# A feed-forward loop that turns half of its features with DMA transposes, as pairs of float16 numbers, in an order written out for four engines

## The chip, the cores and the metric

The kernel runs on one core of a Trainium2 chip. A core has five engines that run side by side, each with its own queue of instructions: TensorE (PE in the profile: matrix products and transposes, with weight loads shown apart as PEld), VectorE (DVE), ScalarE (ACT), GpSimd (POOL) and SyncE (SP, which here only issues DMA transfers). They meet through semaphores. The metric is device time of the whole kernel in microseconds (us), the median of several runs.

## The reference

Two layers of a graph attention followed by a feed-forward part, over 4096 rows of 256 features. The change concerns the feed-forward part of the first layer, which starts from the layer-normed rows and repeats one step thirty times:

```python
def step(h, _):
    h = h + 0.01 * jnp.tanh(h)
    h = h * jax.nn.sigmoid(h)
    h = _layernorm(h, ln_w, ln_b)
    h = jnp.einsum('bsc,dc->bsd', h, W) + b
    return (h, None)
x, _ = jax.lax.scan(step, x, None, length=N_ITERS)   # N_ITERS = 30, 256 features
```

Rows are independent of each other; within a row each step needs the one before. All of it is float32.

## The kernel before, in words

The program is one long function, `gnn_ffn_kernel`: attention of layer 0, the feed-forward stage that is changed here, two attentions of layer 1, and a mixture of experts. Outside of stages with a written order the Tile framework's scheduler decides the order of instructions on each engine.

In the feed-forward stage all 4096 rows stay in SBUF as `y`, at a hundred times their value. They are worked on in 8 groups (`NG`) of 512 rows: 128 partitions by 4 rows (`G`) by 256 features. One group in one step is a unit, so there are 30 x 8 = 240 units, and unit `u` needs the result of unit `u` - 8. The loop over `at` is a software pipeline: one pass starts unit `at`, and carries on with units `at` - 1, `at` - 2 and `at` - 3. A unit goes through these steps:

- ScalarE: tanh of `y` into `th` (L759). GpSimd: `th` + `y` (L760), called the sum below. ScalarE: silu of it into `z` (L765).
- VectorE: mean and variance of the 4 rows of `z` (`over_std`: bn_stats L101, bn_aggr L103), + EPS (L105); GpSimd: to the power -1/2 (L106). The mean itself isn't needed, since `wT` has its own column mean taken off (L741).
- TensorE: 8 transposes of 128x128 that turn `z` (L114, in `transposed`) into PSUM; ScalarE copies them into `zT` (L800).
- TensorE: for each of the 4 rows two float32 products of 128x128 by 128x256, accumulated in PSUM as `po` (L774).
- VectorE: `y` = `po` x rstd + bias, one instruction for each of the 4 rows (L784). In the last step also `t` = 0.01 `y` + `t` (L794), the residual, which is then stored.

`init(g)` (L697 and following) norms the rows of group `g` and scales them into `y`; it runs in the first passes, one group per pass. The weights are prepared on the side, before the loop (L711 to L741).

Of the kernel before, what the change touches and what calls it, by code (L numbers as in the profile page):

```python
# [11 lines left out]
F32 = mybir.dt.float32  # L12
BF16 = mybir.dt.bfloat16
F16 = mybir.dt.float16
I32 = mybir.dt.int32
AF = mybir.ActivationFunctionType
OP = mybir.AluOpType
AX = mybir.AxisListType
# [3 lines left out]
P = 128  # L22
C = 256
KC = C // P
# [3 lines left out]
G = 4  # L28
EPS = 1e-5
# [6 lines left out]
TINY = 1e-30  # L36


def bcast_rows(ap, n=P):

    return bass.AP(tensor=ap.tensor, offset=ap.offset, ap=[[0, n]] + [list(x) for x in ap.ap])
# [3 lines left out]
def gnn_ffn_kernel(ctx: ExitStack, tc: tile.TileContext, a: dict, out: bass.AP):  # L45
    nc = tc.nc
# [3 lines left out]
    NG = NT // G  # L50
    GR = G * P
# [44 lines left out]
    def over_std(pool, src):  # L96

        st = pool.tile([P, G, 6], F32, name="ln_st")
        mv = pool.tile([P, G, 2], F32, name="ln_mv")
        for r in range(G):  # L100
            nc.vector.bn_stats(st[:, r, :], src[:, r, :])  # L101
        for r in range(G):
            nc.vector.bn_aggr(mv[:, r, :], st[:, r, :])  # L103
        rstd = pool.tile([P, G], F32, name="ln_rstd")
        nc.vector.tensor_scalar(rstd, mv[:, :, 1], EPS, None, op0=OP.add)  # L105
        nc.gpsimd.tensor_tensor(rstd, rstd, mhalf, OP.pow)  # L106
        return rstd, mv

    def transposed(psum, src, name="tp"):

        ps = psum.tile([P, KC, GR], F32, name=name)
        for k in range(KC):
            for r in range(G):
                nc.tensor.transpose(ps[:, k, r * P : (r + 1) * P], src[:, r, k * P : (k + 1) * P], ident)  # L114
        return ps
# [560 lines left out]

    with ExitStack() as scope:
        one = scope.enter_context(tc.tile_pool(name="f_one", bufs=1))  # L680
        wT = one.tile([P, KC, C], F32, name="wT")
        bias = one.tile([P, C], F32, name="bias")
        last = one.tile([P, C], F32, name="last")
        y = one.tile([P, NT, C], F32, name="y")
        work = scope.enter_context(tc.tile_pool(name="f_work", bufs=3))
        small = scope.enter_context(tc.tile_pool(name="f_small", bufs=6))

        x1 = {}

        def load(g):  # L690
            if g not in ahead:
                load_ahead(x1d, g)
            x1[g] = ahead.pop(g)

        def init(g):
            t = x1.pop(g)
            rstd, mv = over_std(small, t)  # L697
            rs = small.tile([P, G], F32, name="rs")
            nc.vector.tensor_scalar(rs, rstd, 100.0, None, op0=OP.mult)
            nm = small.tile([P, G], F32, name="nm")  # L700
            nc.vector.scalar_tensor_tensor(nm, mv[:, :, 0], -1.0, rs, op0=OP.mult, op1=OP.mult)
            for r in range(G):
                nc.scalar.activation(
                    y[:, g * G + r, :], t[:, r, :], AF.Identity, scale=rs[:, r : r + 1], bias=nm[:, r : r + 1]
                )

        load(0)
        load(1)
        with tc.tile_pool(name="f_prep", bufs=1) as prep, tc.tile_pool(name="f_pps", bufs=1, space=PSUM) as pps:
            ln = prep.tile([2 * KC, P], F32, name="ln")  # L710
            nc.scalar.dma_start(ln[:KC], a["L0_ffn_ln_w"].rearrange("(k p) -> k p", p=P))  # L711
            nc.scalar.dma_start(ln[KC:], a["L0_ffn_ln_b"].rearrange("(k p) -> k p", p=P))
            wr = prep.tile([P, KC, C], F32, name="wr")
            nc.scalar.dma_start(wr, a["L0_ffn_W"].rearrange("(k p) c -> p k c", p=P))
            nc.scalar.dma_start(bias, bcast_rows(a["L0_ffn_b"]))
            init(0)
            ps = pps.tile([P, 2 * KC], F32, name="ps_ln")
            nc.tensor.transpose(ps, ln, ident[: 2 * KC, : 2 * KC])
            lnT = prep.tile([P, 2 * KC], F32, name="lnT")
            nc.vector.tensor_scalar(lnT, ps, 100.0, None, op0=OP.mult)  # L720
            lbb = prep.tile([P, KC, P], F32, name="lbb")
            nc.vector.tensor_copy(lbb, lnT[:, KC:, None].to_broadcast([P, KC, P]))
            ps = pps.tile([P, KC, C], F32, name="ps_w")
            for k in range(KC):
                for o in range(KC):
                    nc.tensor.transpose(ps[:, k, o * P : (o + 1) * P], wr[:, o, k * P : (k + 1) * P], ident)
            raw = prep.tile([P, KC, C], F32, name="raw")
            nc.vector.tensor_copy(raw, ps)
            ps = pps.tile([P, C], F32, name="ps_b")
            for k in range(KC):  # L730
                nc.tensor.matmul(ps, lbb[:, k, :], raw[:, k, :], start=(k == 0), stop=(k == KC - 1))
            nc.vector.scalar_tensor_tensor(bias, bias, 100.0, ps, op0=OP.mult, op1=OP.add)

            nc.vector.tensor_scalar(last, bias, -100.0, None, op0=OP.add)
            for k in range(KC):
                nc.vector.tensor_scalar(raw[:, k, :], raw[:, k, :], lnT[:, k : k + 1], None, op0=OP.mult)
            ps = pps.tile([P, C], F32, name="ps_m")
            for k in range(KC):
                nc.tensor.matmul(ps, mean, raw[:, k, :], start=(k == 0), stop=(k == KC - 1))
            for k in range(KC):  # L740
                nc.vector.tensor_tensor(wT[:, k, :], raw[:, k, :], ps, OP.subtract)  # L741

        ps_t = scope.enter_context(tc.tile_pool(name="f_pst", bufs=2, space=PSUM))
        ps_o = scope.enter_context(tc.tile_pool(name="f_pso", bufs=2, space=PSUM))

        th, zs, rs, zT = {}, {}, {}, {}
        units = FFN_STEPS * NG
        for at in range(units + 4):
            if at < NG:
                if at + 2 < NG:  # L750
                    load(at + 2)
                if at:
                    init(at)
            if units - NG <= at - 1 < units:
                load((at - 1) % NG)
            if at < units:
                g = at % NG
                th[at] = work.tile([P, G, C], F32, name="th")
                nc.scalar.activation(th[at], y[:, g * G : (g + 1) * G, :], AF.Tanh, scale=0.01)  # L759
                nc.gpsimd.tensor_tensor(th[at], th[at], y[:, g * G : (g + 1) * G, :], OP.add)  # L760
            if 0 <= at - 2 < units:
                pt = transposed(ps_t, zs.pop(at - 2))
            if 0 <= at - 1 < units:
                z = zs[at - 1] = work.tile([P, G, C], F32, name="z", bufs=4)
                nc.scalar.activation(z, th.pop(at - 1), AF.Silu, scale=0.01)  # L765
                rs[at - 1] = over_std(small, z)[0]
            if 0 <= at - 3 < units:
                u = at - 3
                g = u % NG
                src = zT.pop(u)  # L770
                po = ps_o.tile([P, G, C], F32, name="po")
                for r in range(G):
                    for k in range(KC):
                        nc.tensor.matmul(  # L774
                            po[:, r, :],
                            src[:, k, r * P : (r + 1) * P],
                            wT[:, k, :],
                            start=(k == 0),
                            stop=(k == KC - 1),
                        )  # L780
                rstd = rs.pop(u)
                end = u >= units - NG
                for r in range(G):
                    nc.vector.scalar_tensor_tensor(  # L784
                        y[:, g * G + r, :],
                        po[:, r, :],
                        rstd[:, r : r + 1],
                        last if end else bias,
                        op0=OP.mult,
                        op1=OP.add,  # L790
                    )
                if end:
                    t = x1.pop(g)
                    nc.vector.scalar_tensor_tensor(  # L794
                        t, y[:, g * G : (g + 1) * G, :], 0.01, t, op0=OP.mult, op1=OP.add
                    )
                    nc.sync.dma_start(rows_of(x2d, g), t)
            if 0 <= at - 2 < units:
                zT[at - 2] = work.tile([P, KC, GR], F32, name="zT")
                nc.scalar.copy(zT[at - 2], pt)  # L800


    RH = a["L1_ffn_router_w1"].shape[1]
# [456 lines left out]
```

## Time and profile before

| | us |
|---|---|
| median of 3 runs (lowest, highest) | 3557.42 (3556.58, 3568.16) |
| the profiled execution, and its span | 3558.91, 3557.2 |
| feed-forward stage, first tanh to the end of the last L794 | 823.9 to 1905.0 |
| L774 products in the stage: busy, mean of one | 874.1, 0.381 |
| L114 transposes, all of the kernel: busy, mean of one | 250.8, 0.274 |
| L760 sums: busy, mean of one | 567.5, 2.366 |

The profile is one execution taken by the hardware profiler. "Busy" is the time in which an engine had an instruction under way; a line such as "L784 DVE" names the source line and the engine, then the output and inputs with their shapes. What stands in brackets with "<-" is the idle time of the engine just before, and what it waited for. A matmul's duration is modelled and matmuls overlap, so distances from start to start say more than durations; a float32 product has two records.

### The profile page before, as it was taken

What the parts mean: (1) busy time and instruction counts of PE and PEld (TensorE: products, weight loads), DVE (VectorE), ACT (ScalarE), POOL (GpSimd) and SP (SyncE); (2) the same over time, 40 slices, a digit from 0 to 9 for tenths busy, and PEclk for the clock granted to TensorE, in tenths of its full rate; (3) what the DMA queues carried; (4) which work ended last, traced back from release to release, by engine and by line L of the source; (5) the groups of instructions that cost most, each with busy time, mean ns of one, the idle gap of its engine ahead of it and who ended that gap; (6) DMA issues with size and microseconds to landing.
All of it is one profiled execution on the core that took longest, in us unless ns stands there. A gap on an engine that the chain in (4) does not pass through costs nothing. (4 is left out here: it accounts for less than half of the span.)

```text
span 3557.2 us, 80784 instructions
## 1 busy us (share of the span) xinstructions
PE 3272.9 (92%) x33523; PEld 2963.8 (83%) x33523; DVE 3010.9 (85%) x6039; ACT 2613.4 (73%) x2902; POOL 1101.7 (31%) x899
## 2 busy tenths in 40 slices
PE   6889999996999999999998899999979999995995
PEld 5778888885888888888887799999869999993784
DVE  6899999997887877778787799999989999997445
ACT  2688888895766666666663799999879999992221
POOL 3210101004877777777772000000000000001662
PEclk8899999998999999999998899999999999997997
DMA  6796886602000000000006021313221331314224
GB/s 137 139 234 134 196 189 139 189 17 60 1 1 1 1 1 1 1 1 1 1 1 220 14 92 50 123 30 113 79 97 46 111 120 37 120 37 148 90 90 182
DMA packets 280200, 288.47 MB, mean 81 GB/s; under 512 B 97149, under 2 KB 230426, under 8 KB 279834
## 3 DMA queue, kind: packets, MB, share of 16 engines
q1 hardware_dynamic: 198770, 224.18, 19.2%
q0 software_dynamic: 73920, 52.97, 9.7%
q10 hardware_dynamic: 7144, 6.16, 0.6%
q8 instruction: 264, 4.33, 0.5%
q14 instruction: 102, 0.84, 0.1%
HBM read 248.01 MB, written 68.81 MB: 89 GB/s over the span
## 5 line engine op out<-in xcount | busy, mean ns | idle before, releaser
L556 PE MATMUL acc<-vals,m 128*128 128x130 f16 (+1 forms) x19456 | 1723.4, 233 | 83.0 <-DVE m L619 42.7
L470 ACT ACTIVATE st<-f1b,f2b 128x1024 bf16<-128x1024 f32 (+2 forms) x1664 | 1659.4, 1073 | 100.1 <-DVE m L604 92.1
L556 PEld LDWEIGHTS <-m 128*128 128x128 bf16 x19456 | 1518.3, 98 | 181.3 <-DVE m L619 64.9
L604 DVE TENSOR_TENSOR m<-st,m 128x2048 bf16<-128x2048 bf16 (+2 forms) x832 | 929.0, 1134 | 12.4 <-ACT st L470 12.3
L774 PE MATMUL po<-wT,zT 128*128 128x256 f32 x3840 | 874.1, 381 | 13.3 <-ACT zT L800 12.3
L774 PEld LDWEIGHTS po<-wT,zT 128*128 128x128 f32 x3840 | 713.6, 191 | 104.2 <-ACT zT L800 14.8
L556 PE MATMUL acc<-vals,rows 128*128 128x130 f16 x5120 | 614.1, 221 | 15.1 <-DVE rows L619 15.1
L760 POOL TENSOR_TENSOR th<-th,y 128x1024 f32<-128x1024 f32 x240 | 567.5, 2366 | 192.8 <-ACT th L759 192.2
L106 POOL TENSOR_TENSOR ln_rstd<-ln_rstd,mhalf 128x4 f32<-128x4 f32 x272 | 282.4, 1039 | 881.6 <-DVE ln_rstd L105 676.4
L556 PEld LDWEIGHTS <-rows 128*128 128x128 bf16 x5120 | 490.0, 96 | 20.5 <-DVE rows L619 20.1
L101 DVE BATCH_NORM_STATS2 ln_st<-z 128x6 f32<-128x256 f32 x960 | 338.0, 414 | 190.5 <-ACT z L765 190.5
L800 ACT COPY zT<-tp 128x1024 f32<-128x1024 f32 x240 | 242.7, 1011 | 323.8 <-PE tp L114 323.8
L619 DVE TENSOR_TENSOR rows<-m,m 128x2048 bf16<-128x2048 bf16 x320 | 391.7, 1224 | 10.2
L784 DVE SCALAR_TENSOR_TENSOR y<-po,ln_rstd,bias 128x256 f32<-128x256 f32 x928 | 378.8, 470 | 6.6 <-PE po L774 5.9
L765 ACT ACTIVATE z<-th 128x1024 f32<-128x1024 f32 x240 | 254.5, 1060 | 17.4 <-POOL th L760 17.4
L114 PE MATMUL tp<-ident,z 128*128 128x128 f32 x1920 | 250.8, 274 | 8.8 <-ACT z L765 7.9
L114 PEld LDWEIGHTS tp<-ident,z 128*128 128x128 f32 x1920 | 225.3, 141 | 35.5 <-ACT z L765 10.5
L759 ACT ACTIVATE th<-y 128x1024 f32<-128x1024 f32 x240 | 251.3, 1048 | 4.8 <-DVE y L784 4.7
L209 POOL DMA_DIRECT2D rows<-in_adj_dram x80 | 72.9, 912 | 497.3 <-PE tp_m L219 488.2
L619 DVE TENSOR_TENSOR m<-m,m 128x1792 bf16<-128x1792 bf16 (+1 forms) x200 | 202.2, 1011 | 13.0 <-PE acc L556 0.5
L449 POOL MEMSET hs<- 128x4 f32 x3 | 0.3, 102 | 607.2 <-DVE u L500 585.9
L307 PE MATMUL ph<-g_w,xT 128*128 128x264 f32 x384 | 120.0, 477 | 30.9 <-DVE v L377 27.4
(212 smaller groups left out, 2319.7 us busy)
## 6 DMA issues: line engine op xcount, KB each, us to landing
m<-edges SPq DMA_DIRECT2D x32, 2048.0 KB, 9.9
rows<-in_adj_dram POOLq DMA_DIRECT2D x64, 448.0 KB
edges<-ms SPq DMA_DIRECT2D x64, 448.0 KB, 5.0
m<-edges SPq DMA_DIRECT2D x16, 1792.0 KB
f1b<-fd SPq DMA_DIRECT2D x32, 512.0 KB, 3.4
rows<-x1d SPq DMA_DIRECT2D x16, 512.0 KB, 6.3
y<-yd SPq DMA_DIRECT2D x16, 512.0 KB, 9.5
f1b<-fd SPq DMA_DIRECT2D x16, 448.0 KB, 3.3
```

What stands on the lines that cost most here:

```text
L101: nc.vector.bn_stats(st[:, r, :], src[:, r, :])
L106: nc.gpsimd.tensor_tensor(rstd, rstd, mhalf, OP.pow)
L114: nc.tensor.transpose(ps[:, k, r * P : (r + 1) * P], src[:, r, k * P : (k + 1) * P], ident)
L470: nc.scalar.activation(steps[at][:, s, :w], f1b[c, h][:, :w], AF.Relu, bias=f2b[:, 2 * q + s, h : h + 1], scale=BIG)
L556: nc.tensor.matmul(acc[:, i, cols], lhs[:, s, rows], v[:, cols], start=(j == 0 and n_ == 0), stop=(j == NT - 1 and n_ == 1), skip_group_ch ...
L604: nc.vector.tensor_tensor(m1[:, :, :w], st[:, :, :w], m, OP.logical_and if turned(q) else OP.min)
L619: nc.vector.tensor_tensor(m2[:, :, :w], m, m1[:, :, :w], OP.subtract)
L759: nc.scalar.activation(th[at], y[:, g * G : (g + 1) * G, :], AF.Tanh, scale=0.01)
L760: nc.gpsimd.tensor_tensor(th[at], th[at], y[:, g * G : (g + 1) * G, :], OP.add)
L765: nc.scalar.activation(z, th.pop(at - 1), AF.Silu, scale=0.01)
L774: nc.tensor.matmul(po[:, r, :], src[:, k, r * P : (r + 1) * P], wT[:, k, :], start=(k == 0), stop=(k == KC - 1),)
L784: nc.vector.scalar_tensor_tensor(y[:, g * G + r, :], po[:, r, :], rstd[:, r : r + 1], last if end else bias, op0=OP.mult, op1=OP.add,)
```

## The change: half of the features by DMA, and an order by hand

The upper half of the features (128 of 256) is no longer turned by TensorE. ScalarE scales that half of `z` by a power of two and writes it as float16 (`z16[:, 0]`); VectorE computes what the float16 number misses, `z` x scale - upper part, also as float16 (`z16[:, 1]`, the instruction called `lower`). One DMA transpose, issued by SyncE, turns both, 128 partitions by 1024 numbers of two bytes. The weights of that half are likewise split into two float16 numbers (`w16`). The product for a row is then one float32 product for the lower half of the features and four float16 products (two parts by two parts). Before the loop a chain of small instructions finds the two powers of two (`scale`) and their inverse (`under`), by which GpSimd multiplies rstd in an instruction of its own.

The loop's instructions stand in `tc.manual_schedule` for TensorE, VectorE, ScalarE and GpSimd: these run in the order in which the text has them. The pipeline is deeper: a pass carries on with units `at` - 2 to `at` - 5. GpSimd's sum gets one more wait (`add_manual_dep`): it waits for `lower` of the same pass. The statistics of `init` are taken a pass ahead (`measure`).

```diff
-        wT = one.tile([P, KC, C], F32, name="wT")
+        wT = one.tile([P, C], F32, name="wT")
+        w16 = one.tile([P, 2, C], F16, name="w16")
+        scale = one.tile([P, 2], F32, name="scale")
+        under = one.tile([P, G], F32, name="under")
...
+        def measure(g):
+            measured[g] = over_std(small, x1[g])
...
-            rstd, mv = over_std(small, t)
+            rstd, mv = measured.pop(g)
...
-        load(0)
-        load(1)
+        for g in range(3):
+            load(g)
...
+            measure(0)
             init(0)
+            measure(1)
...
             for k in range(KC):
-                nc.vector.tensor_tensor(wT[:, k, :], raw[:, k, :], ps, OP.subtract)
+                nc.vector.tensor_tensor(raw[:, k, :], raw[:, k, :], ps, OP.subtract)
+            sq = prep.tile([P, KC, C], F32, name="sq")
+            nc.vector.tensor_tensor(sq, raw, raw, OP.mult)
...
+            nc.gpsimd.tensor_tensor(far[:, 1:2], far[:, 0:1], mhalf[:, :1], OP.pow)
...
+            nc.vector.tensor_scalar(wT, raw[:, 0, :], scale[:, :1], scale[:, 1:], op0=OP.mult, op1=OP.mult)
+            nc.vector.tensor_scalar(w16[:, 0, :], raw[:, 1, :], scale[:, 1:], None, op0=OP.mult)
+            nc.vector.scalar_tensor_tensor(
+                w16[:, 1, :], raw[:, 1, :], scale[:, 1:], w16[:, 0, :], op0=OP.mult, op1=OP.subtract
+            )
...
+        with tc.manual_schedule(engines={PE, DVE, Activation, Pool}):   # written out in full in the code
+            for at in range(units + 6):
+                if at + 3 < NG:
+                    load(at + 3)
+                u = at - 3
+                if 0 <= u < units:
+                    z = zs.pop(u)
+                    pt = ps_t.tile([P, GR], F32, name="tp")
+                    for r in range(G):
+                        nc.tensor.transpose(pt[:, r * P : (r + 1) * P], z[:, r, :P], ident)
+                u = at - 5
+                if 0 <= u < units:
+                    g = u % NG
+                    po, rstd = pos.pop(u), rs.pop(u)
+                    end = u >= units - NG
+                    for r in range(G):
+                        nc.vector.scalar_tensor_tensor(
+                            y[:, g * G + r, :], po[:, r, :], rstd[:, r : r + 1],
+                            last if end else bias, op0=OP.mult, op1=OP.add,
+                        )
+                u = at - 2
+                lower = None
+                if 0 <= u < units:
+                    z = zs[u] = work.tile([P, G, C], F32, name="z")
+                    nc.scalar.activation(z, th.pop(u), AF.Silu, scale=0.01)
+                    z16 = work.tile([P, 2, G, P], F16, name="z16", bufs=4)
+                    nc.scalar.activation(z16[:, 0], z[:, :, P:], AF.Identity, scale=scale[:, :1])
+                    lower = nc.vector.scalar_tensor_tensor(
+                        z16[:, 1], z[:, :, P:], scale[:, :1], z16[:, 0], op0=OP.mult, op1=OP.subtract
+                    )
+                    zT16[u] = work.tile([P, 2 * G, P], F16, name="zT16", bufs=4)
+                    nc.sync.dma_start_transpose(zT16[u], z16.rearrange("p s r c -> p (s r c)"))
+                if at < units:
+                    g = at % NG
+                    th[at] = work.tile([P, G, C], F32, name="th", bufs=4)
+                    nc.scalar.activation(th[at], y[:, g * G : (g + 1) * G, :], AF.Tanh, scale=0.01)
+                    ins = nc.gpsimd.tensor_tensor(th[at], th[at], y[:, g * G : (g + 1) * G, :], OP.add)
+                    if lower is not None:
+                        tc.add_manual_dep(ins.ins, lower.ins.name, ..., reason="the port that both use")
+                if 0 <= u < units:
+                    st = small.tile([P, G, 6], F32, name="z_st")
+                    mv = small.tile([P, G, 2], F32, name="z_mv")
+                    for r in range(G):
+                        nc.vector.bn_stats(st[:, r, :], z[:, r, :])
+                    for r in range(G):
+                        nc.vector.bn_aggr(mv[:, r, :], st[:, r, :])
+                    rs[u] = small.tile([P, G], F32, name="z_rs")
+                    nc.vector.tensor_scalar(rs[u], mv[:, :, 1], EPS, None, op0=OP.add)
+                    nc.gpsimd.tensor_tensor(rs[u], rs[u], mhalf, OP.pow)
+                    nc.gpsimd.tensor_tensor(rs[u], rs[u], under, OP.mult)
+                u = at - 3
+                if 0 <= u < units:
+                    zT[u] = work.tile([P, GR], F32, name="zT")
+                    nc.scalar.copy(zT[u], pt)
+                if at + 1 < NG:
+                    init(at + 1)
+                if at + 2 < NG:
+                    measure(at + 2)
+                u = at - 4
+                if 0 <= u < units:
+                    src, src16 = zT.pop(u), zT16.pop(u)
+                    po = pos[u] = ps_o.tile([P, G, C], F32, name="po")
+                    for r in range(G):
+                        nc.tensor.matmul(po[:, r, :], src[:, r * P : (r + 1) * P], wT, start=True, stop=False)
+                        for part in range(2):
+                            for other in range(2):
+                                nc.tensor.matmul(
+                                    po[:, r, :], src16[:, part * G + r, :], w16[:, other, :],
+                                    start=False, stop=(part == 1 and other == 1),
+                                )
+                    if u >= units - NG:
+                        load(u % NG)
...
```

What is left out of the diff: the old loop, which the section on the kernel before shows; the small instructions of the scales; and the end of the loop, where the residual of unit `at` - 5 is added and stored as before.

More of the change, by code (lines that the diff above doesn't have):

```diff
@@ L693, in load @@
             x1[g] = ahead.pop(g)
+        measured = {}
+        def measure(g):
+            measured[g] = over_std(small, x1[g])
         def init(g):
             t = x1.pop(g)
-            rstd, mv = over_std(small, t)
+            rstd, mv = measured.pop(g)
             rs = small.tile([P, G], F32, name="rs")
@@ L740, in gnn_ffn_kernel @@
             for k in range(KC):
-                nc.vector.tensor_tensor(wT[:, k, :], raw[:, k, :], ps, OP.subtract)
+                nc.vector.tensor_tensor(raw[:, k, :], raw[:, k, :], ps, OP.subtract)
+            sq = prep.tile([P, KC, C], F32, name="sq")
+            nc.vector.tensor_tensor(sq, raw, raw, OP.mult)
+            ps = pps.tile([P, C], F32, name="ps_m")
+            for k in range(KC):
+                nc.tensor.matmul(ps, mean, sq[:, k, :], start=(k == 0), stop=(k == KC - 1))
+            far = prep.tile([P, 4], F32, name="far")
@@ new lines, in gnn_ffn_kernel @@
+            nc.vector.tensor_reduce(far[:, 0:1], ps, axis=AX.X, op=OP.max)
+            nc.vector.tensor_scalar(far[:, 0:1], far[:, 0:1], TINY, None, op0=OP.add)
+            nc.gpsimd.tensor_tensor(far[:, 1:2], far[:, 0:1], mhalf[:, :1], OP.pow)
+            nc.vector.tensor_tensor(far[:, 1:2], far[:, 1:2], far[:, 0:1], OP.mult)
+            nc.vector.tensor_reduce(far[:, 2:3], bias, axis=AX.X, op=OP.max, apply_absolute_value=True)
+            big = prep.tile([P, 2], F32, name="big")
+            nc.vector.tensor_scalar(big[:, 1:2], far[:, 1:2], math.sqrt(C), None, op0=OP.mult)
@@ new lines, in gnn_ffn_kernel @@
+            nc.vector.scalar_tensor_tensor(
+                far[:, 3:4], big[:, 1:2], math.sqrt(C), far[:, 2:3], op0=OP.mult, op1=OP.add
+            )
+            nc.vector.tensor_scalar(far[:, 3:4], far[:, 3:4], 0.01, 0.01, op0=OP.mult, op1=OP.add)
+            nc.vector.tensor_scalar(big[:, :1], far[:, 3:4], math.sqrt(C) + 0.1, None, op0=OP.max)
+            bits = prep.tile([P, 2], I32, name="bits")
+            nc.vector.tensor_scalar(bits, big.bitcast(I32), 23, None, op0=OP.arith_shift_right)
@@ new lines, in gnn_ffn_kernel @@
+            nc.vector.tensor_scalar(
+                scale.bitcast(I32), bits, -(2.0**23), (2 * 127 + 14) * 2.0**23, op0=OP.mult, op1=OP.add
+            )
+            inv = prep.tile([P, 2], F32, name="inv")
+            nc.vector.tensor_scalar(
+                inv.bitcast(I32), bits, 2.0**23, -14 * 2.0**23, op0=OP.mult, op1=OP.add
+            )
+            nc.vector.tensor_tensor(
+                under, inv[:, :1].to_broadcast([P, G]), inv[:, 1:].to_broadcast([P, G]), OP.mult
+            )
@@ L743, in gnn_ffn_kernel @@
+            nc.vector.tensor_scalar(wT, raw[:, 0, :], scale[:, :1], scale[:, 1:], op0=OP.mult, op1=OP.mult)
+            nc.vector.tensor_scalar(w16[:, 0, :], raw[:, 1, :], scale[:, 1:], None, op0=OP.mult)
+            nc.vector.scalar_tensor_tensor(
+                w16[:, 1, :], raw[:, 1, :], scale[:, 1:], w16[:, 0, :], op0=OP.mult, op1=OP.subtract
+            )
         ps_t = scope.enter_context(tc.tile_pool(name="f_pst", bufs=2, space=PSUM))
         ps_o = scope.enter_context(tc.tile_pool(name="f_pso", bufs=2, space=PSUM))
-        th, zs, rs, zT = {}, {}, {}, {}
+        th, zs, rs, zT, zT16, pos = {}, {}, {}, {}, {}, {}
@@ L747, in gnn_ffn_kernel @@
         units = FFN_STEPS * NG
-        for at in range(units + 4):
-            if at < NG:
-                if at + 2 < NG:
[L751 to L792, printed above, removed]
@@ new lines, in gnn_ffn_kernel @@
+        with tc.manual_schedule(
+            engines={
+                mybir.EngineType.PE,
+                mybir.EngineType.DVE,
+                mybir.EngineType.Activation,
+                mybir.EngineType.Pool,
+            }
+        ):
+            for at in range(units + 6):
[13 more added lines that the diff above has]
+                    for r in range(G):
+                        nc.vector.scalar_tensor_tensor(
+                            y[:, g * G + r, :],
+                            po[:, r, :],
+                            rstd[:, r : r + 1],
+                            last if end else bias,
+                            op0=OP.mult,
+                            op1=OP.add,
+                        )
+                u = at - 2
[7 more added lines that the diff above has]
+                        z16[:, 1], z[:, :, P:], scale[:, :1], z16[:, 0], op0=OP.mult, op1=OP.subtract
+                    )
+                    zT16[u] = work.tile([P, 2 * G, P], F16, name="zT16", bufs=4)
[6 more added lines that the diff above has]
+                    if lower is not None:
+                        tc.add_manual_dep(
+                            ins.ins,
+                            lower.ins.name,
+                            mybir.DependencyInfo(mybir.DependencyClass.Sync, mybir.DependencyReason.DATA),
+                            reason="the port that both use",
+                        )
+                if 0 <= u < units:
[15 more added lines that the diff above has]
+                    init(at + 1)
+                if at + 2 < NG:
+                    measure(at + 2)
[8 more added lines that the diff above has]
+                                nc.tensor.matmul(
+                                    po[:, r, :],
+                                    src16[:, part * G + r, :],
+                                    w16[:, other, :],
+                                    start=False,
+                                    stop=(part == 1 and other == 1),
+                                )
+                    if u >= units - NG:
+                        load(u % NG)
+                u = at - 5
+                if units - NG <= u < units:
+                    g = u % NG
@@ L797, in gnn_ffn_kernel @@
                     nc.sync.dma_start(rows_of(x2d, g), t)
-            if 0 <= at - 2 < units:
-                zT[at - 2] = work.tile([P, KC, GR], F32, name="zT")
-                nc.scalar.copy(zT[at - 2], pt)
     RH = a["L1_ffn_router_w1"].shape[1]
```

## The prediction

> **What bounds the kernel now.** I read the page's header and slices first, then the stretches of the feed-forward stage, then its groups, then its order in time. The stage runs from the first tanh at 823.9 us to the last scaled addition (L794), which ends at 1905.0 us: 1081 us for 240 units (30 steps by 8 groups of 512 rows). The stretches view says who is busy there (columns: busy us of each engine, granted clock, DMA share, GB/s):
>
> ```profile
> core 0: us, PE busy (x) PEld busy (x) DVE busy (x) ACT busy (x) POOL busy (x), PEclk, DMA share, GB/s
> 860.00:1000.00 140.00, 130.33 (x695) 113.44 (x695) 114.28 (x435) 99.97 (x109) 115.05 (x70) 0.98 0.05 16
> 1000.00:1800.00 800.00, 800.00 (x4437) 714.62 (x4436) 637.55 (x2403) 538.28 (x556) 625.44 (x370) 1.00 0.00 1
> ```
>
> TensorE has no idle time at all, at full clock, and DMA carries nothing. VectorE and GpSimd are at 80% and 78%. The sums of GpSimd (L760) start 4.329 us apart on average. TensorE accounts for this exactly: successive L774 matmul records start 0.2156 us apart (256 columns; each float32 product is two records) and successive transposes L114 0.1097 us, so a unit is 16 x 0.2156 + 8 x 0.1097 = 4.33 us. TensorE is the bound.
>
> The order in time, two units (start us, us, engine, line, operation):
>
> ```profile
> 1303.25 2.36 POOL L760 TENSOR_TENSOR th<-th,y 128x1024 f32<-128x1024 f32 x1 [0.84 <-ACT th L759]
> ...
> 1303.52 0.36 DVE L103 BATCH_NORM_AGGREGATE ln_mv<-ln_st 128x2 f32<-128x6 f32 x4
> 1303.80 1.63 DVE L784 SCALAR_TENSOR_TENSOR y<-po,ln_rstd,bias 128x256 f32<-128x256 f32 x4
> ...
> 1305.34 0.30 DVE L105 TENSOR_SCALAR ln_rstd<-ln_mv 128x4 f32<-128x4 f32 x1
> ...
> 1305.72 1.02 POOL L106 TENSOR_TENSOR ln_rstd<-ln_rstd,mhalf 128x4 f32<-128x4 f32 x1
> ...
> 1306.53 1.41 DVE L101 BATCH_NORM_STATS2 ln_st<-z 128x6 f32<-128x256 f32 x4 [0.89 <-ACT z L765]
> ...
> 1307.58 2.36 POOL L760 TENSOR_TENSOR th<-th,y 128x1024 f32<-128x1024 f32 x1 [0.84 <-ACT th L759]
> ...
> 1309.98 0.16 DVE L105 TENSOR_SCALAR ln_rstd<-ln_mv 128x4 f32<-128x4 f32 x1
> ```
>
> The line to look at is L105, four additions per partition. At 1309.98 it takes 0.16 us; the sum before it had ended at 1309.94. At 1305.34 it takes 0.30, and ends 0.03 after the sum that ends at 1305.61. Of the 224 L105 in the stage from 905 to 1865 us, 218 start while an L760 runs, and every one ends 0.024 to 0.034 us after that L760; the other six take 0.156 to 0.168. It is worse where the sum has longer to go:
>
> ```profile
> 825.17 2.44 DVE L734 TENSOR_SCALAR last<-bias 128x256 f32<-128x256 f32 x1
> ...
> 852.80 2.01 DVE L105 TENSOR_SCALAR ln_rstd<-ln_mv 128x4 f32<-128x4 f32 x1
> ```
>
> So GpSimd's 2.36 us sum holds VectorE's tensor_scalar up, whole. L784 and L103 run through a sum without growing (four L784 in 1.63). Today this costs nothing, since VectorE waits 0.89 us for ACT's z in every unit anyway.
>
> **What the Trainium skill says.** "SBUF — State Buffer", Who interferes with whom: VectorE and GpSimd share a port pair by an exclusive lock; a tensor_scalar in a two-port mode, or a VectorE instruction with two SBUF inputs beside a GpSimd one that reads SBUF, blocks fully until the other ends; an instruction with one SBUF input is untouched. The trace agrees (0.16 against 0.30 and 2.01; L784 has po in PSUM and only bias in SBUF). Both transpose prices below are from the skill; no run here shows a DMA transpose.
>
> **The change part by part.** A loop is one pass over `at`.
> - TensorE: 4 transposes 0.439, 8 records of float32 products 1.725, and 16 float16 products of 256 columns. Half of all successive L556 float16 matmuls (130 columns, each with its own weight load) start 0.0555 us apart, 0.43 ns a column, so 256 columns take 0.109 and 16 take 1.75. Sum 3.91 us, 0.42 less than now.
> - ScalarE: z and tanh stay (1.06 and 1.05), the copy zT halves to about 0.6, the new float16 copy is about 0.6. 3.3 us, not the bound. It runs nearly a loop ahead, so z16 and tanh are there when wanted.
> - VectorE: start to start, four bn_stats take 1.32, four aggregates 0.28, L784 1.54, a free L105 0.08: 3.22. New is `lower`, 128x512 with two SBUF inputs: L661, a scalar_tensor_tensor of that size, takes 0.69 (about 0.61 start to start). Sum 3.83: by busy time it fits.
> - GpSimd: sum 2.36, pow 1.02, a new 128x4 product about 0.2 (L332, 128x16, is 0.22): 3.6, fits.
> - SP: one transpose of 256 KB per loop. The skill gives 1309 ns for 128x128 ("VectorE: DVE Perf Modes", The three transpose paths), estimated 10.5 us for eight if nothing overlaps, and 261 GB/s effective ("DMA: Bandwidth & Descriptors", Latency and other measured facts), estimated 1.0 us. I take 2 to 4 us with latency, since 1309 ns looks like a latency of one small transfer. From `lower` to the matmul that needs it lie two loops, some 8 us to spare. Hidden; above 8 us it shows.
> - The written order. VectorE's queue in a loop is L784 x4, `lower`, bn_stats, aggregates, the +EPS tensor_scalar. GpSimd's sum now waits for `lower`, so it starts 0.08 after it (the delay from L105 to L106) and lasts 2.365. The +EPS is ready 1.60 after `lower` has left, but the sum is only some 1.5 us in. It is the same instruction as L105, so it waits for the sum's end, and the next L784 and `lower` are queued behind it. Nothing on this ring can overlap: `lower` 0.69, delay 0.08, sum 2.365, and from the sum's end to the next L784 -0.055 (+0.026 to the end of +EPS, -0.08 pipelining), four L784 1.54. That is **4.62 us a loop**, against 3.9 for each engine's own work and 4.33 now. Pow and product (1.3 us after the sum) just fit under L784; if not, 0.1 more.
> - Start. Until now wT is ready at 829.9. Squares, maximum, pow and some dozen tiny operations of about 0.2 each follow, some held by sums: `lower` of unit 0 at about 839 (estimate). Loops 2 to 5 also carry init and measure: 0.61+0.16+2.365+0.03+0.30+1.68 = 5.1, plus 1.54 from loop 5 on, where L784 comes in; loop 6 has no measure. `lower` of loop 7 falls at about 868.
> - Steady: 234 loops from 7 to 241 at 4.62 = 1081, to 1949. The drain (statistics, three loops of L784 and L794 without sums) is about 10, and five L794 of 1.2 inside loops with sums 6. End 1965, against 1905.0: **+60 us**.
> - Around it nothing moves: the same order in the attention before and after, the x2d stores and loads at the end as now.
>
> The profiled execution took 3558.9 us (span 3557.2), 1.5 above the median 3557.42 of the runs. +60 on the median gives 3617; I say 3618.
>
> **Rivals.**
> 1. The ring does not close (faster). If neither +EPS nor `lower` were held by GpSimd, a loop would be 3.9, TensorE's: 234 x 0.72 = 168 less, 3450. If +EPS is free but `lower` has to wait for pow and product, the loop is 0.69+0.08+2.365+1.3 = 4.4 or less, down to 4.2 where they overlap partly: 3520 to 3567. It ends below today when a loop is under 4.62 - 60/234 = 4.36. For it: float16 products are cheap and all engines have room. Against it: 218 of 218.
> 2. The DMA transposes are the bound (slower still). A transfer of 5 to 6 us gives (0.4 to 1.4) x 240 on top of 3618, 3710 to 3950; eight serial ones 10.5 us, about 5030. For it: no trace here bounds them. Against it: DMA is idle in the stage.
> 3. The ring closes, but front and fill save what it costs: within 0.3% of now. It needs a loop of 4.33 to 4.40.
>
> **How the numbers follow.** A change of 0.3%, 11 us, is about what a measurement of this kernel can tell from none. The ring: 0.72, its own range 3595 to 3670 (a loop of 4.55 to 4.8). Faster by rival 1: 0.15. Same: 0.05. Bound by transposes: 0.08. So faster 0.15, same 0.05, slower 0.80. The range must leave out no more than 2 in 10: 3530 leaves out the lower two thirds of rival 1, 3690 most of rival 2.
>
> **What would show it.** Right: sums 4.6 us apart; the +EPS about 1 us long and ending 0.03 after each sum; the sum released by `lower`; TensorE with about 0.7 us idle per loop, waiting for L784's buffer. Wrong: +EPS at 0.16 us throughout, or TensorE without idle time (rival 1); TensorE waiting for the DMA, or `lower` for a z16 buffer (rival 2). float16 products further apart than 0.11 would show weight loads that aren't hidden: at 0.2 TensorE's loop is 5.4.

## The result, and the profile after

The changed kernel takes 3668.22 us (median of four runs, 3667.17 to 3668.88) against 3562.79 for the kernel before beside it: 1.0296 times the time, interval 1.0273 to 1.0319, 105 us slower. The forecast was 3618, in a range of 3530 to 3690. Direction and cause were forecast; the change was put at 60 us, and it is 105.

The feed-forward stage of the profiled execution runs from 822.9 to 2006.3 us, 1183 us, where it took 1081: 102 us more. The stretch view of the changed kernel (columns as before):

```profile
core 0: us, PE busy (x) PEld busy (x) DVE busy (x) ACT busy (x) POOL busy (x), PEclk, DMA share, GB/s
...
1000.00:1800.00 800.00, 699.28 (x4713) 544.61 (x4711) 794.27 (x2356) 538.35 (x674) 600.98 (x506) 1.00 0.32 56
```

TensorE has fallen from 800 busy us to 699, VectorE has risen from 638 to 794. But not all of VectorE's 794 is work. The order in time, VectorE alone:

```profile
1301.01 0.74 DVE L837 SCALAR_TENSOR_TENSOR z<-z,scale,z 128x512 f16<-128x512 f32 x1
1301.67 1.39 DVE L858 BATCH_NORM_STATS2 z_st<-z 128x6 f32<-128x256 f32 x4
1302.98 0.36 DVE L860 BATCH_NORM_AGGREGATE z_mv<-z_st 128x2 f32<-128x6 f32 x4
1303.37 0.90 DVE L862 TENSOR_SCALAR z_rs<-z_mv 128x4 f32<-128x4 f32 x1
1304.19 1.65 DVE L822 SCALAR_TENSOR_TENSOR y<-po,z_rs,bias 128x256 f32<-128x256 f32 x4
1305.76 0.73 DVE L837 SCALAR_TENSOR_TENSOR z<-z,scale,z 128x512 f16<-128x512 f32 x1
```

and GpSimd over the same time:

```profile
1301.89 2.36 POOL L846 TENSOR_TENSOR th<-th,y 128x1024 f32<-128x1024 f32 x1 [0.99 <-DVE z L837]
1304.35 1.02 POOL L863 TENSOR_TENSOR z_rs<-z_rs,mhalf 128x4 f32<-128x4 f32 x1
1305.44 0.20 POOL L864 TENSOR_TENSOR z_rs<-z_rs,under 128x4 f32<-128x4 f32 x1
```

L862 is +EPS (L105 before): four additions per partition, 0.90 us, where the free one took 0.16. The sum L846 ends at 1304.25 and L862 at 1304.27. Of all 240 L862, 238 start during a sum and end 0.024 to 0.030 us after it. The ring can be read off these lines: `lower` (L837) at 1301.01, sum from 1301.89 to 1304.25, L822 from 1304.19, the next `lower` at 1305.76: 4.75 us. The waits of the same kernel from 1000 to 1800 us (what waited for what, us in total, times, longest):

```profile
ACT z L834 <- POOL th L846: 257.6, 169, 1.8
POOL th L846 <- DVE z L837: 161.8, 163, 1.0
PEld po L878 <- ACT z L834: 135.6, 168, 1.1
PE po L878 <- DVE y L822: 100.6, 168, 0.9
```

The third line is a weight load whose releaser is inferred; TensorE's own wait is the fourth, 0.60 us a loop for a PSUM buffer that L822 frees. The wait of L862 stands in no line: here the time for which an instruction is held counts as its busy time. The 168 L862 of this stretch are busy for 152 us; at 0.16 each they would take 27 (estimate).

### The profile page after: what moved, and what is told of

It is laid out like the page before. It is cut to its first block, busy times and chain, and to the rows that moved or that the text cites. A ratio compares the mean times of both kernels' runs of the same rounds, so it can differ in the third digit from the quotient of the medians.

```text
span 3667.1 us, 84398 instructions
## 1 busy us (share of the span) xinstructions
PE 3231.3 (88%) x34487; PEld 2813.9 (77%) x34487; DVE 3312.1 (90%) x6295; ACT 2680.5 (73%) x3142; POOL 1153.5 (31%) x1140
## 5 line engine op out<-in xcount | busy, mean ns | idle before, releaser
L878 PE MATMUL po<-wT,zT 128*128 128x256 f32 x1920 | 593.6, 391 | 150.5 <-DVE y L822 142.8
L846 POOL TENSOR_TENSOR th<-th,y 128x1024 f32<-128x1024 f32 x240 | 565.4, 2356 | 247.6 <-DVE z L837 223.8
L881 PE MATMUL po<-w,zT 128*128 128x256 f16 x3840 | 578.4, 273 | 0.0
L881 PEld LDWEIGHTS <-zT 128*128 128x128 f16 x3840 | 376.8, 98 | 161.4 <-issue 1.7
L878 PEld LDWEIGHTS po<-wT,zT 128*128 128x128 f32 x1920 | 290.3, 191 | 209.1 <-ACT z L834 184.1
L822 DVE SCALAR_TENSOR_TENSOR y<-po,z_rs,bias 128x256 f32<-128x256 f32 x928 | 382.1, 470 | 0.0
L858 DVE BATCH_NORM_STATS2 z_st<-z 128x6 f32<-128x256 f32 x960 | 334.2, 406 | 0.0
L106 POOL TENSOR_TENSOR ln_rstd<-ln_rstd,mhalf 128x4 f32<-128x4 f32 x32 | 37.9, 1185 | 847.0 <-DVE ln_rstd L105 846.9
L863 POOL TENSOR_TENSOR z_rs<-z_rs,mhalf 128x4 f32<-128x4 f32 x240 | 247.8, 1033 | 30.8 <-DVE z_rs L862 5.9
L862 DVE TENSOR_SCALAR z_rs<-z_mv 128x4 f32<-128x4 f32 x240 | 216.0, 900 | 8.2
```

The lines of the kernel that those rows point to most:

```text
L822: nc.vector.scalar_tensor_tensor(y[:, g * G + r, :], po[:, r, :], rstd[:, r : r + 1], last if end else bias, op0=OP.mult, op1=OP.add,)
L846: ins = nc.gpsimd.tensor_tensor(th[at], th[at], y[:, g * G : (g + 1) * G, :], OP.add)
L858: nc.vector.bn_stats(st[:, r, :], z[:, r, :])
L863: nc.gpsimd.tensor_tensor(rs[u], rs[u], mhalf, OP.pow)
L878: nc.tensor.matmul(po[:, r, :], src[:, r * P : (r + 1) * P], wT, start=True, stop=False)
L881: nc.tensor.matmul(po[:, r, :], src16[:, part * G + r, :], w16[:, other, :], start=False, stop=(part == 1 and other == 1),)
```

## The experiments

Each run has its own runs of the kernel before beside it, on its chip; ratios are to those.

### e1: the statistics in PSUM, so that +EPS is not held

```diff
-                    mv = small.tile([P, G, 2], F32, name="z_mv")
+                    mv = ps_v.tile([P, G, 2], F32, name="z_mv")     # a PSUM pool of two
```

> Edit: the aggregated statistics (z_mv) lie in PSUM instead of SBUF, so the +EPS tensor_scalar has no SBUF input; nothing else. Theory of the ring (+EPS is held by GpSimd's sum through the shared port): +EPS takes about 0.2 us and no longer ends with the sum; the next L822 starts some 0.9 earlier; then `lower` comes up against pow (1.01) and waits for it: a loop of 0.88 + 2.36 + 0.07 + 1.01 = 4.3 to 4.4 (if the product with `under` slips in ahead of `lower`, 4.6), so 3575 to 3635. Rival (the hold of +EPS is not what sets the loop, something else as late does): sums stay 4.75 apart, 3668.

Measured 3596.07 us against 3548.68: 1.0134 (1.0116 to 1.0153), a loop of 4.51. +EPS is free: all 155 between 1000 and 1700 us start inside a sum, end before it does and take 0.161 to 0.164 us. So the hold did set the loop. But what follows it is not what I expected. VectorE in this run, with the sum of the same loop:

```profile
1303.27 1.40 DVE L858 BATCH_NORM_STATS2 z_st<-z 128x6 f32<-128x256 f32 x4
...
1303.50 2.36 POOL L846 TENSOR_TENSOR th<-th,y 128x1024 f32<-128x1024 f32 x1 [0.90 <-DVE z L837]
...
1304.59 0.85 DVE L860 BATCH_NORM_AGGREGATE z_mv<-z_st 128x2 f32<-128x6 f32 x4
...
1305.48 0.16 DVE L862 TENSOR_SCALAR z_rs<-z_mv 128x4 f32<-128x4 f32 x1
1305.56 1.66 DVE L822 SCALAR_TENSOR_TENSOR y<-po,z_rs,bias 128x256 f32<-128x256 f32 x4
```

The four aggregates, which overlap in 0.36 us when they write to SBUF, take 0.85 when they write to PSUM. The cure brings 0.5 us of its own, and VectorE's chain without any hold is then 4.5 us. The time fell into my span by luck, for another reason than the one given with it: `lower` doesn't wait for pow, and the aggregates happen to cost about as much as that wait would have.

### e2: the sum does not wait for `lower`

```diff
-                    if lower is not None:
-                        tc.add_manual_dep(ins.ins, lower.ins.name, ..., reason="the port that both use")
```

> Edit: GpSimd's sum no longer waits for `lower`; nothing else. Port theory: the sum starts as soon as pow and product are done, `lower` comes up against it and is held for most of 2.36; ring from sum to sum: `lower` 0.66 after the sum, statistics 1.60, +EPS 0.1, delay 0.08, pow 1.01, product 0.27, delay 0.07, sum 2.36 = 6.15 us a loop, about 4000 us. Rival (the port does not matter, the added wait itself costs): sums 4.2 or less apart, 3540 or faster.

Measured 3943.9 us in a single run, a loop of 6.01, near the 6.15 of the port theory. VectorE, then GpSimd:

```profile
1300.14 0.17 DVE L855 TENSOR_SCALAR z_rs<-z_mv 128x4 f32<-128x4 f32 x1
1300.22 1.66 DVE L822 SCALAR_TENSOR_TENSOR y<-po,z_rs,bias 128x256 f32<-128x256 f32 x4
1301.79 2.73 DVE L837 SCALAR_TENSOR_TENSOR z<-z,scale,z 128x512 f16<-128x512 f32 x1
```

```profile
1300.38 1.01 POOL L856 TENSOR_TENSOR z_rs<-z_rs,mhalf 128x4 f32<-128x4 f32 x1 [2.43 <-DVE z_rs L855]
1301.47 0.20 POOL L857 TENSOR_TENSOR z_rs<-z_rs,under 128x4 f32<-128x4 f32 x1
1301.62 2.35 POOL L846 TENSOR_TENSOR th<-th,y 128x1024 f32<-128x1024 f32 x1
```

Now the sum gets the port first, and `lower` takes 2.73 us instead of 0.74. +EPS is free at 0.17. The added wait is worth 1.26 us a loop; it moves the hold from `lower` to +EPS, where it is shorter, and does not remove it.

### e3: the written order without the float16 split

The new order, depth and early statistics stay; the products are as before:

```diff
-                    pt = ps_t.tile([P, GR], F32, name="tp")
-                    for r in range(G):
-                        nc.tensor.transpose(pt[:, r * P : (r + 1) * P], z[:, r, :P], ident)
+                    pt = transposed(ps_t, z)
...
-                    z16 = ...; lower = ...; nc.sync.dma_start_transpose(...); tc.add_manual_dep(...)
-                    nc.gpsimd.tensor_tensor(rs[u], rs[u], under, OP.mult)
...
+                        for k in range(KC):
+                            nc.tensor.matmul(po[:, r, :], src[:, k, r * P : (r + 1) * P], wT[:, k, :], ...)
```

> Edit: the written order, the deeper pipeline and the early statistics stay; the float16 split is undone (TensorE turns all features, float32 products, no `lower`, no DMA transpose, no wait of the sum, no product with `under`). If the split makes the loss: TensorE bound again, 4.33 a loop, +EPS hidden; 3545 to 3575, as the kernel before. If the order makes it: a loop of 4.6 or more, 3630 or more.

Measured 3544.54 us against 3548.68: 0.9987 (0.9980 to 0.9994), a loop of 4.329, TensorE busy throughout. The order by itself costs nothing; its 0.13% is too small to build on. The loss comes with the split.

### e4: neither instruction at the port

```diff
+                    zp = ps_v.tile([P, G, P], F32, name="zp")
+                    nc.scalar.copy(zp, z[:, :, P:])
                     lower = nc.vector.scalar_tensor_tensor(
-                        z16[:, 1], z[:, :, P:], scale[:, :1], z16[:, 0], op0=OP.mult, op1=OP.subtract
+                        z16[:, 1], zp, scale[:, :1], z16[:, 0], op0=OP.mult, op1=OP.subtract
                     )
```

with z_mv in PSUM as in e1, and without the sum's wait as in e2.

> Edit: neither VectorE instruction needs the shared port: z_mv in PSUM, and ScalarE puts a second copy of the upper half of z into PSUM, from which `lower` reads (z16 is its only SBUF input); the sum no longer waits for `lower`. Port theory: no hold is left; ScalarE 3.9, TensorE 3.9, VectorE 3.9 to 4.0 and GpSimd 3.7 set a loop of 4.0 to 4.1: 3490 to 3520, faster than both kernels. Rival (one of these engines, or the DMA transposes, is the bound whatever the port does): a loop of 4.4 or more, above 3580.

Measured 3595.28 us against 3548.68: 1.0127 (1.0108 to 1.0146), a loop of 4.51, the same as e1. My 3490 to 3520 was wrong: I didn't count with the slow aggregates, which this kernel shares with e1 (0.85 us here as well). It says nothing against the split, only that PSUM is the wrong place for z_mv.

The trace also holds the counterpart of e2. Here too the sum comes first and `lower` (L839) starts inside it, but `lower` now has one of its two inputs in PSUM:

```profile
1301.17 2.36 POOL L848 TENSOR_TENSOR th<-th,y 128x1024 f32<-128x1024 f32 x1
1301.35 0.74 DVE L839 SCALAR_TENSOR_TENSOR z<-zp,scale,z 128x512 f16<-128x512 f32 x1
```

It is not held: all 155 between 1000 and 1700 us start inside a sum and take 0.739 to 0.744 us. In e2, with both inputs in SBUF, all 117 do so and take 2.72 to 2.74. Where its input lies decides whether `lower` is held.

### e6: +EPS on ScalarE

```diff
-                    rs[u] = small.tile([P, G], F32, name="z_rs")
-                    nc.vector.tensor_scalar(rs[u], mv[:, :, 1], EPS, None, op0=OP.add)
-                    nc.gpsimd.tensor_tensor(rs[u], rs[u], mhalf, OP.pow)
-                    nc.gpsimd.tensor_tensor(rs[u], rs[u], under, OP.mult)
+                    mvs[u] = mv
                 u = at - 3
                 if 0 <= u < units:
+                    rs[u] = small.tile([P, G], F32, name="z_rs")
+                    nc.scalar.activation(rs[u], mvs.pop(u)[:, :, 1], AF.Identity, bias=eps)
+                    nc.gpsimd.tensor_tensor(rs[u], rs[u], mhalf, OP.pow)
+                    nc.gpsimd.tensor_tensor(rs[u], rs[u], under, OP.mult)
```

> Edit: +EPS is taken from VectorE and done by ScalarE[...], with pow and the product one pass later; the statistics stay in SBUF, the sum still waits for `lower`. VectorE's own work is then 3.9 a loop, without the slower aggregates of e1. Port theory: the next VectorE instruction that meets GpSimd is `lower`, held by pow: 0.88 + 2.36 + 0.07 + 1.01 = 4.3 to 4.4 a loop, 4.6 if the product slips in ahead: about 3560 to 3625. If the port sets nothing once +EPS is gone: 3.95 to 4.1, about 3480 to 3510.

Measured **3460.57 us against 3549.41: 0.9753 (0.9737 to 0.9769)**. Moving one instruction of four elements per partition to another engine, with pow and the product a pass later, turns 3% slower into 2.5% faster. The delay of pow and product isn't tried alone; e1, which frees +EPS without it, shortens the loop too. The loop is 3.92, and the stretch view shows TensorE without idle time again:

```profile
1000.00:1700.00 700.00, 700.00 (x5002) 573.29 (x5002) 698.15 (x2324) 642.07 (x894) 669.03 (x536) 1.00 0.39 68
```

VectorE is nearly as full; that TensorE sets the loop is seen in e5 below, where VectorE is less busy and the loop is no shorter. ScalarE's +EPS (L867) runs inside a sum (L848) in 0.30 us:

```profile
1298.40 2.37 POOL L848 TENSOR_TENSOR th<-th,y 128x1024 f32<-128x1024 f32 x1
...
1299.88 0.30 ACT L867 ACTIVATE z_rs<-z_mv,eps 128x4 f32<-128x4 f32 x1 [0.25 <-DVE z_mv L862]
```

This is the second of the two expectations, and more than it asked for; my port theory had bet on the first. What it had wrong is seen here:

```profile
1300.71 1.02 POOL L868 TENSOR_TENSOR z_rs<-z_rs,mhalf 128x4 f32<-128x4 f32 x1
...
1301.43 0.74 DVE L839 SCALAR_TENSOR_TENSOR z<-z,scale,z 128x512 f16<-128x512 f32 x1
1301.81 0.41 POOL L869 TENSOR_TENSOR z_rs<-z_rs,under 128x4 f32<-128x4 f32 x1
```

`lower` (L839) starts inside the pow L868 and takes its usual 0.74 us: 176 of 178 do so between 1000 and 1700 us, all with 0.736 to 0.747. Pow does not hold it. These start 0.4 to 0.7 us after the pow; that its beginning doesn't hold either is seen in the first loops of the changed kernel, where a small instruction with two SBUF inputs (L713, in `init`) starts 0.03 us after a pow, five times, and takes 0.18 us:

```profile
858.56 1.01 POOL L863 TENSOR_TENSOR z_rs<-z_rs,mhalf 128x4 f32<-128x4 f32 x1
858.59 0.18 DVE L713 SCALAR_TENSOR_TENSOR nm<-ln_mv,rs 128x4 f32<-128x4 f32 x1
```

The one L713 that starts inside a sum takes 2.24 us. The other way round the hold is there (e6 again): the product L869 starts inside `lower` and ends 0.06 after it, at 0.41 instead of 0.20. So the time that a GpSimd instruction is shown as busy is not the time for which it keeps VectorE from the port. The sum does for its whole length, pow hardly or not at all; why is not shown.

### e5 and e7: further down the same road

e5 is e6 with three more edits: `lower` reads from PSUM as in e4, the sum doesn't wait, and ScalarE's +EPS takes in the factor `under`:

```diff
-                    nc.scalar.activation(rs[u], mvs.pop(u)[:, :, 1], AF.Identity, bias=eps)
-                    nc.gpsimd.tensor_tensor(rs[u], rs[u], mhalf, OP.pow)
-                    nc.gpsimd.tensor_tensor(rs[u], rs[u], under, OP.mult)
+                    nc.scalar.activation(rs[u], mvs.pop(u)[:, :, 1], AF.Identity, scale=over[:, :1], bias=over[:, 1:])
+                    nc.gpsimd.tensor_tensor(rs[u], rs[u], mhalf, OP.pow)
```

> Edit: as e6, and `lower` reads its z from a second copy in PSUM, so that it has one SBUF input; the factor `under` is folded into ScalarE's scale and offset, so GpSimd has only sum and pow; the sum no longer waits for `lower`. Port theory: nothing on VectorE meets GpSimd any more; TensorE 3.91, VectorE 3.85 to 3.95 and ScalarE 3.9 set a loop of 3.95 to 4.1: 3480 to 3515, clearly faster than the kernel before. Rival (the split is bound elsewhere, for example by the DMA transposes or the PSUM buffers): a loop of 4.3 or more, 3555 or more.

Measured 3467.28 us against 3549.41: 0.9769 (0.9753 to 0.9785), a loop of 3.93. No gain over e6: with +EPS gone TensorE sets the loop, and nothing that is done for VectorE and GpSimd beyond that is seen. TensorE is without idle time here too:

```profile
1000.00:1700.00 700.00, 700.00 (x4989) 573.57 (x4987) 691.95 (x2316) 694.21 (x1070) 594.78 (x357) 1.00 0.38 68
```

e7 moves `init` to the head of a pass:

```diff
+                if at + 1 < NG:
+                    init(at + 1)
                 u = at - 3
...
-                if at + 1 < NG:
-                    init(at + 1)
```

> Edit: as e5, and init of the next group stands at the head of a pass instead of behind the sum. In the changed kernel the first loops take 7.5 us because init waits for the +EPS and so for the sum, and ScalarE's silu and z16 stand behind it. Theory: 6 loops shorter by 1 to 2 us each, 5 to 12 us faster than e5. Rival (the front is bound by other work): no difference.

Measured 3476.89 us against 3549.41: 0.9798 (0.9782 to 0.9815), slower than e5. The loops of the front, the first ones, which also carry `init`, grow from 8.0 to 10.1 us, though there are fewer of them. The theory of the front falls in this form, and the two traces say why. In e5 +EPS is off VectorE, but the front isn't free: the first instruction of `init` (L711, a multiplication of four numbers per partition) now meets the sum in its place, takes 1.21 us instead of 0.17, and ends 0.03 us after the sum:

```profile
857.92 2.36 POOL L845 TENSOR_TENSOR th<-th,y 128x1024 f32<-128x1024 f32 x1 [2.54 <-ACT th L844]
...
859.09 1.21 DVE L711 TENSOR_SCALAR rs<-ln_rstd 128x4 f32<-128x4 f32 x1
```

In e7 `init` comes right after `measure` of the same group, whose pow (L106) stands in GpSimd's queue behind the sum and the loop's own pow. L711 waits for it:

```profile
862.49 0.17 DVE L711 TENSOR_SCALAR rs<-ln_rstd 128x4 f32<-128x4 f32 x1 [1.25 <-POOL ln_rstd L106]
```

So the edit put a longer wait in the place of the hold. A front without either wasn't run.

### e8: +EPS on ScalarE in the kernel before

```diff
-            nc.vector.tensor_scalar(rstd, mv[:, :, 1], EPS, None, op0=OP.add)
+            nc.scalar.activation(rstd, mv[:, :, 1], AF.Identity, bias=eps)
```

for the loop's statistics alone.

> Edit, on the kernel before: +EPS of the loop is done by ScalarE instead of VectorE; nothing else. In the kernel before GpSimd's sum holds +EPS just the same, but TensorE sets the loop. Theory: the hold costs nothing there, so a loop stays at 4.33 and the time within 0.3% (3540 to 3560). Rival (+EPS on VectorE costs in any kernel): 0.5% or more faster, 3530 or less.

Measured 3559.46 us against 3558.78: 1.0006 (0.9997 to 1.0014). The hold of the same instruction costs nothing where TensorE sets the loop. It is shorter there, 0.14 us (0.30 against 0.16), and VectorE has room: with +EPS gone, its wait for ScalarE's z grows from 0.89 to 1.10 us.

```profile
1303.09 1.41 DVE L101 BATCH_NORM_STATS2 ln_st<-z 128x6 f32<-128x256 f32 x4 [1.10 <-ACT z L770]
```

### e9: a shorter sum

```diff
-                    ins = nc.gpsimd.tensor_tensor(th[at], th[at], y[:, g * G : (g + 1) * G, :], OP.add)
+                    ins = nc.gpsimd.tensor_tensor(th[at][:, :3], th[at][:, :3], y[:, g * G : g * G + 3, :], OP.add)
```

> Edit, on the changed kernel: GpSimd's sum covers three of the four rows of a group (128x768 instead of 128x1024). This leaves out a quarter of the addition of y to tanh, so the result is another one. One size of the ring is changed by about 0.58 us (a quarter of 2.36). Ring theory: a loop shorter by the same 0.55 to 0.6, 4.15 to 4.2 us, some 130 us faster than the changed kernel: about 3520. Rival (the loop is set by another chain): 4.6 to 4.75 a loop, 3620 or more.

Measured 3534.31 us against 3558.78: 0.9926 (0.9910 to 0.9943). The sum is 0.543 us shorter (1.813 against 2.356), the loop 0.541 (4.205 against 4.746, medians). GpSimd, with the same wait ahead of the sum as in the changed kernel:

```profile
1300.54 1.81 POOL L846 TENSOR_TENSOR th<-th,y 128x768 f32<-128x768 f32 x1 [0.99 <-DVE z L837]
...
1304.74 1.82 POOL L846 TENSOR_TENSOR th<-th,y 128x768 f32<-128x768 f32 x1 [0.99 <-DVE z L837]
```

The sum is on the ring with its whole length, one to one, and +EPS follows it: between 1000 and 1700 us all 166 start inside a sum and end 0.025 to 0.033 us after it.

## Why the prediction was right, and where it was not

**The bound before, and what the parts cost.** TensorE's estimate of 3.91 us a loop after the change was right: float16 products start 0.109 us apart, weight loads hidden, and e6 and e5, where TensorE is the bound, run at 3.92 and 3.93. The DMA transposes were put at 2 to 4 us and hidden: they take 3.0 us from issue to landing (median; the longest 4.2), and SP 1.24 us to issue. This lies between the two estimates made from the Trainium skill's prices (1.0 from "DMA: Bandwidth & Descriptors", Latency and other measured facts; 10.5 from "VectorE: DVE Perf Modes", The three transpose paths). The assumption that 1309 ns for one 128x128 is mostly latency fits this, but no run tests it. The changed kernel moves 56 GB/s in the loop at a DMA share of 0.32. TensorE has no wait for a transpose among its waits.

**The ring.** The step that decided the prediction, +EPS held by the sum because the sum now starts right behind `lower`, is shown four ways: 238 of 240 in the trace; e1 and e6, which free +EPS in two manners and shorten the loop; e9, where the loop follows the sum; e2, where the hold moves to `lower`. Its size was 4.62 and is 4.75. Three of its terms were too small, `lower`, the delay behind it and the step from L822 to the next `lower`:

| term of the ring | put at | measured |
|---|---|---|
| `lower` | 0.69 (from L661, all float32) | 0.74 |
| delay from `lower` to the sum | 0.08 (from L105 to pow) | 0.14 |
| sum | 2.365 | 2.36 |
| end of the sum to L822 | -0.055 | -0.06 |
| L822 to the next `lower` | 1.54 | 1.57 |
| sum of them | 4.62 | 4.75 |

Over 234 loops that is 30 us of the 41 by which the end of the stage was missed (1965 forecast, 2006.3 in the profile). The delay of 0.08 was taken from another pair of instructions; 0.14 stood in the profile of before too, between the end of a tanh (1303.11) and the start of the sum that it releases (1303.25):

```profile
1302.06 1.05 ACT L759 ACTIVATE th<-y 128x1024 f32<-128x1024 f32 x1
```

**The front.** `lower` of loop 7 was put at 868 and is at 877.6: 10 of the 41. The loops that also carry `init` take 7.5 us and not 5.1 to 6.6. I had summed VectorE's queue alone. In the trace ScalarE's part of init (2.07 us) waits for the +EPS hold to end, silu and z16 stand behind it, and `lower` waits for z16. Freeing +EPS alone hardly helps here, 7.4 us a loop in e6: as in e5 above, the first instruction of `init` meets the sum in its place. The drain took 12 and not 10.

**Outside the stage.** From the end of the stage to the end of the kernel the two profiled executions differ by 9 us (1661 against 1652), with the same instructions. The other runs of this study have 1640 to 1657 there. It is not explained.

**The rivals.** Rival 1 had two halves. Its ground, that float16 products are cheap and all engines have room, was right: e6 is that case at last, 89 us under its kernel before where rival 1 had 107. Its other half, that +EPS free would still leave 4.2 to 4.4 with `lower` behind pow, was wrong, and so was the same step in the expectations of e1 and e6: pow does not hold `lower`. Rivals 2 and 3 did not come about.

The change's own gain was there all along: 0.41 us a loop on TensorE, about 96 us over 234 loops. It was taken back, and twice over, by a four-element addition that costs 0.8 us a loop (4.75 against 3.92), 0.74 of it spent held by the sum.

## What to carry to other kernels

Before speeding up the engine that bounds a loop, look for instructions on the others whose duration varies with what a neighbour does; a hold that costs nothing in slack can grow, and become the bound, when the slack goes (e8 against e6). Follow it as a ring: write down what each held instruction waits for and what is queued behind it, since the profile shows it as busy time and not as a wait. And when a wait is added to keep two instructions apart, ask which instruction meets the same neighbour next: here the smallest one on the engine. The same holds when a held instruction is taken away, as the first loops of e5 show.

## What was not expected of the hardware

- Four bn_aggr that write to PSUM take 0.85 us instead of 0.36 (e1, e4): 0.186 each, one after the other, where in SBUF they overlap.
- GpSimd's pow of 128x4 is shown for 1.01 us and does not hold up a VectorE instruction with two SBUF inputs (176 in e6 started inside one, none was longer than usual), while the sum of 128x1024 holds +EPS and such an instruction until it ends (2.73 instead of 0.74 us in e2). With +EPS's input or one of `lower`'s two in PSUM the sum holds neither (0.16 us in e1, 0.74 in e4). The Trainium skill ("SBUF — State Buffer", Who interferes with whom) has the pair held for the whole instruction; for the sum the runs agree, for pow they do not.
- VectorE holds GpSimd as well: the product with `under` takes 0.41 instead of 0.20 us when it starts inside `lower` (e6).
